# Routed expert slots: down products one slot later, up weights in halves, TensorE's order as called

## The chip, the cores and the metric

One core of a Trainium2 chip runs the whole program. The time is device microseconds of one execution. The engines are TensorE (PE: matrix products and transposes by a product with the identity), VectorE (DVE), ScalarE (ACT), GpSimd (POOL) and SyncE (SP), which here only sends transfers; ScalarE and GpSimd send some too. Each engine works through its own list of instructions in order, and waits there for what its next instruction needs.

## The reference, cut to what matters

A two-layer decoder on 4 x 512 tokens of width 512, each layer with gated cross attention and a gated feed-forward part. The part at stake is the first layer's feed-forward part, a mixture of experts: each token goes to its two best experts of 8, scaled by its score.

```python
scores = softmax(xf @ gate_w)                       # xf: 2048 x 512
_, sel = top_k(scores + expert_bias, 2)
order = argsort(sel.reshape(-1), stable=True)       # 4096 rows, by expert
token_idx = order // 2
routed_in = xf[token_idx] * top_scores_sorted[:, None]
h = silu(ragged_dot(routed_in, w1, counts)) * ragged_dot(routed_in, w3, counts)
routed_out = ragged_dot(h, w2, counts)              # w1, w3: 8 x 512 x 448, w2: 8 x 448 x 512
out = (silu(xf @ sw1) * (xf @ sw3)) @ sw2
out = out.at[token_idx].add(routed_out)
```

The second layer (a grouped attention with weights that were rounded to fp8, and a feed-forward part with weights of -1, 0 and 1) comes after it. Its weights are made ready while the slots run, and that is all of it that meets the change.

## The kernel before, in words

Tokens are scattered in DRAM to 39 slots of 128 rows, so that a slot's rows all belong to one expert (`owners` holds which). A loop runs over the slots; each slot `s` goes through four products on TensorE:

- `turn_in(s)` transposes the slot's rows: four 128x128 transposes into one PSUM tile of `ps_m` (2 buffers), copied to SBUF by `k.evac`. This helper gives its copies to VectorE (L120) and ScalarE (L122) in turn.
- `up(s)` multiplies them with the expert's two up matrices, tile `w13` (512 rows in four chunks of 128, times 2 x 448 columns, 1792 KB; two tiles, used by even and by odd slots): four chunks times two matrices, fp32, each as two passes. ScalarE takes the Silu of one result (L908), VectorE multiplies the other in (L909, the gate).
- `turn_hidden(s)` transposes the 448 hidden columns in four pieces of 112, with the same helper for the copy.
- `down(s)` multiplies with the expert's down matrix, tile `w2` (896 KB, two tiles). ScalarE scales the result into `m_y` (L927) and sends it to `slots_out` in DRAM (L928).

`load(s)` reads the slot's expert into a register of SP and sends for `w13`; `load_down(s)` sends for `w2`. Both are conditional from the third slot on: nothing is moved when slot `s - 2`, which used the same tile, had the same expert. So large transfers come only where an expert ends: with the loads of slots 0, 1, 16, 17, 18, 33 and 34. `load_rows(s)` sends for a slot's rows on ScalarE's queue, four slots ahead, into one of 7 buffers.

At the end of each round the loop calls steps of two lists of other work, which the second layer needs:

- `split`: steps that load a raw weight chunk (L1084, on SP), scale it (L1074), centre it (L1052 to L1054) on VectorE, round it on ScalarE (L1078), subtract on GpSimd (L1079), and store both halves by SP (L1080). One or two a slot.
- `ternary`: steps that load a 704 KB piece `t_raw` (L1807, on SP) and reduce it (L1814), two steps that make a scale from it with a small matmul (`t_pm`, L1824), and steps that turn a piece into codes (L1837 to L1839 on VectorE, a store by SP, L1840).

The order in which these calls become each engine's list is in most places that of a scheduler, which moves instructions where dependencies allow; in the attention stages a wrapper `Ordered` holds an engine's instructions in the order of the calls. In the slots of the kernel before, no such wrapper is used. There TensorE's list has early slots in the order hidden turn, row turn, up, down; late slots in the order up, hidden turn, row turn, down.

After the slots the program gathers each token's two rows from `slots_out`, adds them to `k.x`, and goes on to `context` (L989), the second layer's first products.

Of the kernel before, what the change touches and what calls it, by code (L numbers as in the profile page):

```python
# [22 lines left out]
P = 128  # L23
# [4 lines left out]
KC = D // P  # L28
# [5 lines left out]
E, HID, HC = 8, 448, 112  # L34
NHC = HID // HC
SLOTS = (2 * T + E * (P - 1)) // P
# [33 lines left out]
class Kernel:  # L70


    def __init__(self, ctx, tc, a, out):
        self.tc, self.nc, self.a, self.out = tc, tc.nc, a, out
        self.flip = 0
        nc = self.nc
        const = ctx.enter_context(tc.tile_pool(name="const", bufs=1))
        self.const = const
        self.small = ctx.enter_context(tc.tile_pool(name="small", bufs=4))

        self.x = const.tile([P, NT, D], F32, name="x_res")
        self.pcol = const.tile([P, NCOLS], F32, name="pcol_sb")
        self.rows = const.tile([P, NROWS], F32, name="rows_sb")
        nc.sync.dma_start(self.pcol, a["pcol"])
        nc.sync.dma_start(self.rows, a["rows"].partition_broadcast(P))

        self.ident = const.tile([P, P], F32, name="ident")
        make_identity(nc, self.ident)
        self.identb = const.tile([P, P], BF, name="identb")
        nc.vector.tensor_copy(self.identb, self.ident)  # L90
        self.ones = const.tile([P, P], F32, name="ones")
        nc.gpsimd.memset(self.ones, 1.0)
        self.neghalf = const.tile([P, 8], F32, name="neghalf")
        nc.gpsimd.memset(self.neghalf, -0.5)
        self.tg = const.tile([P, 4], F32, name="tg")
        nc.scalar.activation(self.tg, self.row("gates"), AF.Tanh)
# [534 lines left out]
        line.drain()  # L631


def moe(k, split, codes8, scratch, ffn):


# [9 lines left out]
    nc, tc, a = k.nc, k.tc, k.a  # L646
    with ExitStack() as ctx:
# [12 lines left out]
        w13 = [p1.tile([P, KC, 2, HID], F32, name=f"m_w13_{j}") for j in range(2)]  # L660
# [38 lines left out]
        for b in range(B):  # L699
            k.layernorm([(xn[b][:, t, :], k.x[:, b * TB + t, :]) for t in range(TB)])  # L700
            for c in range(KC):
                pt = ps_m.tile([P, S], F32, tag="ps_m")
# [44 lines left out]
        def by_token(name):  # L747
            return p1.tile([P, NT], F32, name=name)
# [34 lines left out]
        pt = ps_m.tile([P, 2, NT, E], F32, tag="ps_m", name="r_counts")  # L783
# [41 lines left out]
        for r, hot in enumerate(hots):  # L825
# [8 lines left out]
            s = by_token(f"r_s{r}")  # L834
# [22 lines left out]
        got = {}  # L857

        def load(s):


            e = got["e", s] = nc.values_load(
                owners[:, s : s + 1], engines=(mybir.EngineType.SP,), min_val=0, max_val=E - 1,
                skip_runtime_bounds_check_because="it is at most E - 1 by construction",
            )
            got["new", s] = None if s < 2 else e != got["e", s - 2]
            nc.sync.dma_start(w13[s % 2], a["w13"][e], cond=got["new", s])

        def load_rows(s):
            work = p6.tile([P, 4, D], F32, tag="m_big", name=f"m_work{s}")  # L870
            rows = nc.scalar.dma_start(work[:, 0, :], rows_in[ts(s, P), :])
            for scatter in scatters:
                tc.add_manual_dep(
                    rows.ins, scatter.name,
                    mybir.DependencyInfo(mybir.DependencyClass.Sync, mybir.DependencyReason.DATA),
                    reason="any of them may write a row of the slot",
                )

            tc.add_manual_dep(
                rows.ins, silus[B * NHC - NHC - 1].name,  # L880
                mybir.DependencyInfo(
                    mybir.DependencyClass.NoSync, mybir.DependencyReason.SCHED_ONLY
                ),
                reason="order of ScalarE's queue",
            )
            got["work", s] = work

        def load_down(s):
            nc.sync.dma_start(w2[s % 2], a["w2"][got["e", s]], cond=got["new", s])

        def turn_in(s):
            work = got["work", s]
            pt = ps_m.tile([P, KC, P], F32, tag="ps_m")
            for c in range(KC):
                nc.tensor.transpose(pt[:, c, :], work[:, 0, ts(c, P)], k.ident)
            k.evac(work[:, 1, :].rearrange("p (c t) -> p c t", c=KC), pt)

        def up(s):
            work, w = got["work", s], w13[s % 2]
            pu = ps_h.tile([P, HID], F32, tag="ps_h")  # L900
            pw = ps_h.tile([P, HID], F32, tag="ps_h")
            for c in range(KC):
                for half, pp in enumerate((pu, pw)):
                    nc.tensor.matmul(
                        pp, lhsT=work[:, 1, ts(c, P)], rhs=w[:, c, half, :],
                        start=(c == 0), stop=(c == KC - 1),
                    )
            nc.scalar.activation(work[:, 2, 0:HID], pu, AF.Silu)  # L908
            nc.vector.tensor_tensor(work[:, 2, 0:HID], work[:, 2, 0:HID], pw, ALU.mult)  # L909

        def turn_hidden(s):
            work = got["work", s]
            pt = ps_m.tile([P, NHC, P], F32, tag="ps_m")
            for m in range(NHC):
                nc.tensor.transpose(pt[:HC, m, :], work[:, 2, ts(m, HC)], k.ident)
            k.evac(work[:HC, 3, :].rearrange("p (c t) -> p c t", c=NHC), pt[:HC])

        def down(s):
            work, w = got.pop(("work", s)), w2[s % 2]
            po = ps_o.tile([P, D], F32, tag="ps_o")  # L920
            for m in range(NHC):
                nc.tensor.matmul(
                    po, lhsT=work[:HC, 3, ts(m, P)], rhs=w[:, m, :],
                    start=(m == 0), stop=(m == NHC - 1),
                )
            y = p4.tile([P, D], F32, tag="m_row", name=f"m_y{s}")
            nc.scalar.activation(y, po, AF.Copy, scale=k.tg[:, 2:3])  # L927
            nc.scalar.dma_start(rows_out[ts(s, P), :], y)  # L928
# [4 lines left out]
        for s in range(2):  # L933
            load(s)
            load_down(s)
        turn_in(0)
        up(0)
        turn_in(1)
        for s in range(SLOTS):
            if s + 1 < SLOTS:  # L940
                up(s + 1)
            turn_hidden(s)
            if s + 2 < SLOTS:
                load(s + 2)
                turn_in(s + 2)
            down(s)
            if s + 2 < SLOTS:
                load_down(s + 2)
            if s + 4 < SLOTS:
                load_rows(s + 4)  # L950
            for _ in range(-(-len(split) // (SLOTS - s))):
                split.pop(0)(ps)
            if ternary:
                ternary.pop(0)()


        kaff = p1.tile([P, 2], F32, name="kx_affine")
# [99 lines left out]
def split_weights(k):  # L1057
# [49 lines left out]
        steps += [partial(key_value, i, c) for c in range(KC)]  # L1107
        steps += [partial(project, i, src, h) for src in range(2) for h in range(HP)]
    return s, steps


class Ordered:


    def __init__(self, tc, engine):
        self.tc, self.engine = tc, engine

    def __getattr__(self, name):
        call = getattr(self.engine, name)
        return lambda *args, **kw: self.tc.keep_in_program_order(call(*args, **kw))  # L1120


class Beat:
# [16 lines left out]
    def load(self, tick, engine):  # L1140
        return self.loads.get((tick, engine), 0)
# [712 lines left out]
@with_exitstack  # L1854
def kernel(ctx: ExitStack, tc: tile.TileContext, a: dict, out: bass.AP):
    k = Kernel(ctx, tc, a, out)
    xattn_int8(k)
    scratch, split = split_weights(k)
    with tc.tile_pool(name="codes", bufs=1) as pool:
        codes8 = Codes(k, pool)  # L1860
        ffn = Ffn(k)
        first = moe(k, split, codes8, scratch, ffn)
        attend_and_feed(k, scratch, codes8, first, ffn)
# [85 lines left out]
```

## Time and profile before

| what | us |
|---|---|
| median of 3 runs | 3661.64 (3653.7 to 3664.58) |
| the profiled execution | 3658.38 |
| its span, first to last instruction | 3656.7 |
| mean granted TensorE clock | 0.965 |
| slot stage, first row turn to last down product (starts) | 868.6 to 1311.62 |

Times in the profile are from the start of the span. A line of the timeline gives the start, the duration, the engine, the line of the program, the operation, what it writes and reads, its shape and how many instructions of the kind follow one another; a bracket gives the idle time just before it and what ended it. A matmul's end is modelled, so of a row of matmuls the distance between starts is the better measure of their pace. "SPq" is SP's own queue, where a transfer's line gives the time at which it was sent, not how long it was under way. An fp32 product shows as two instructions.

### The profile page before, as it was taken

Reading aid. Unit: us, or ns where it says so; the run is one execution under the profiler, and the core shown is the slowest. Engines: PE = TensorE matmul, PEld = TensorE weight load, DVE = VectorE, ACT = ScalarE, POOL = GpSimd, SP = SyncE. Lnnn points to the kernel's source line nnn. Section 1 sums busy time; section 2 is a strip of 40 time slices with the busy share of each in tenths; the row PEclk is TensorE's granted clock in tenths of the full one; section 3 lists DMA queues with packets and bytes.
Section 4 is the critical chain, followed back from the end, with each engine's and each line's share of the span. In section 5 each row is a group of like instructions: output and inputs, shape, how many; then the busy total and the mean of one; then the engine's idle time right before and its main releaser. Section 6 shows DMA issues by size and latency. Waiting matters only on the chain.

```text
span 3656.7 us, 46871 instructions
## 1 busy us (share of the span) xinstructions
PE 3350.2 (92%) x15536; PEld 2193.1 (60%) x15552; DVE 2208.1 (60%) x4678; ACT 1507.4 (41%) x4198; POOL 1345.1 (37%) x1517
## 2 busy tenths in 40 slices
PE   6988987889999878889999999999999999999996
PEld 3544544434544433347777777776777777777774
DVE  6676676642143345635557767678766687666555
ACT  2544554111212211126555455554555554555542
POOL 1000000331001134524446654457545466544442
PEclk8999998989999989999999999999999999999998
DMA  5544442476265563343333242322332332332310
GB/s 179 153 113 113 121 110 60 173 242 215 104 208 174 203 225 115 134 140 100 103 104 104 81 141 90 121 96 94 117 124 90 116 104 98 113 110 95 105 50 14
DMA packets 223025, 452.85 MB, mean 124 GB/s; under 512 B 21440, under 2 KB 80320, under 8 KB 220224
## 3 DMA queue, kind: packets, MB, share of 16 engines
q1 hardware_dynamic: 206432, 412.62, 34.5%
q10 hardware_dynamic: 11232, 20.45, 1.7%
q0 software_dynamic: 5120, 16.78, 1.4%
q8 instruction: 125, 2.05, 0.2%
q14 instruction: 116, 0.95, 0.1%
HBM read 420.87 MB, written 116.98 MB: 147 GB/s over the span
## 4 chain that ended last, share of the span: by engine, by line
PE 47%; DVE 8%; POOL 2%; issue 2%; DMA 1%; ACT 1%; SPq 0%; DVEq 0%; POOLq 0%; ACTq 0%
PE ps_w L1120 10%; PE pss L1120 10%; PE ps_p L1120 9%; PE ps_o L1120 9%; PE ps_t L1120 7%; PE pk L989 2%; DVE y L1120 2%; DMA m_got<-slots_out,r_posi 1%; DVE nm L1120 1%; DVE g_hn L1120 1%; DVE t_work L1120 1%; DVE e L1120 1%; DVE g_pT L1120 1%; DVE t_sm L1120 0%; POOL g_rstd L1120 0%
## 5 line engine op out<-in xcount | busy, mean ns | idle before, releaser
L1120 PEld LDWEIGHTS ps_w<-g_pT,g_v 128*128 128x128 f32 x2048 | 388.1, 190 | 298.9 <-issue 222.2
L1120 PE MATMUL ps_w<-g_pT,g_v 128*128 128x256 f32 x2048 | 529.3, 381 | 23.3 <-DVE y L1120 12.5
L1120 ACT ACTIVATE g_p<-pss,nm 128x512 f32<-128x512 f32 x512 | 350.9, 685 | 479.0 <-DVE nm L1120 434.2
L1120 PE MATMUL pss<-g_kT,g_qT 128*128 128x512 f32 x1024 | 524.1, 594 | 0.9 <-ACT g_p L1120 0.9
L1120 POOL TENSOR_SCALAR g_p<-g_p,rs 128x512 f32<-128x512 f32 x512 | 368.6, 721 | 385.3 <-DVE rs L1120 366.1
L1120 DVE TENSOR_REDUCE nm<-pss 128x1 f32<-128x512 f32 x512 | 351.1, 686 | 105.7 <-PE pss L1120 104.5
L1120 PE MATMUL ps_t<-ident,g_p 128*128 128x128 f32 x2048 | 307.5, 273 | 0.0
L1120 PE MATMUL ps_o<-g_wp,g_cq 128*128 128x512 f32 x1024 | 286.4, 422 | 5.6 <-POOL g_cq L1120 3.0
L1079 POOL TENSOR_TENSOR hl<-raw,hl 128x512 fp32r<-128x512 f32 x80 | 102.0, 1282 | 512.0 <-ACT hl L1078 501.0
L1120 POOL TENSOR_TENSOR g_rstd<-ss,neghalf 128x4 f32<-128x4 f32 (+1 forms) x192 | 178.2, 928 | 303.8 <-ACT ss L1120 303.6
L1120 PE MATMUL ps_p<-g_wq,g_xq 128*128 128x512 f32 x1024 | 282.2, 417 | 6.5 <-DMA g_wq<-s_q 6.2
L1120 DVE COPY g_pT<-ps_t 128x512 f32<-128x512 f32 x246 | 168.4, 685 | 166.9 <-PE ps_t L1120 166.5
L1120 POOL TENSOR_TENSOR t<-y,c 128x512 f32<-128x512 bf16 x176 | 204.9, 1164 | 162.9 <-DVE c L1120 84.4
L1120 PEld LDWEIGHTS ps_t<-ident,g_p 128*128 128x128 f32 x2048 | 243.8, 141 | 26.0 <-POOL g_p L1120 0.9
L1120 ACT COPY g_pT<-ps_t 128x512 f32<-128x512 f32 x266 | 155.0, 583 | 231.6 <-PE ps_t L1120 231.2
L989 PE MATMUL pk<-m_wx,m_ctxT 128*128 128x512 f32 x512 | 239.7, 613 | 5.2 <-issue 5.2
L521 ACT ACTIVATE p<-pss,nm 128x512 f32<-128x512 f32 x256 | 175.4, 690 | 135.9 <-DVE nm L518 134.6
L1120 PEld LDWEIGHTS ps_o<-g_wp,g_cq 128*128 128x128 f32 x1024 | 195.8, 192 | 48.5 <-POOL g_cq L1120 3.5
L1120 PEld LDWEIGHTS ps_p<-g_wq,g_xq 128*128 128x128 f32 x1024 | 191.4, 190 | 50.0 <-issue 7.9
L518 DVE TENSOR_REDUCE nm<-pss 128x1 f32<-128x512 f32 x256 | 173.2, 688 | 71.0 <-PE pss L513 69.6
L1120 DVE RECIPROCAL rs<-g_sm 128x1 f32<-128x1 f32 x512 | 82.5, 161 | 205.2 <-ACT g_p L1120 203.2
L1120 ACT ACTIVATE junk<-ps_p 128x128 f32<-128x128 f32 x640 | 177.1, 277 | 67.3 <-PE ps_p L1120 53.1
(312 smaller groups left out, 6017.5 us busy)
## 6 DMA issues: line engine op xcount, KB each, us to landing
m_w<-in_w_dram SPq DMA_DIRECT2D x39, 1792.0 KB
g_wp<-s_proj SPq DMA_DIRECT2D x128, 512.0 KB
m_w<-in_w_dram SPq DMA_DIRECT2D x39, 896.0 KB
g_wq<-s_q SPq DMA_DIRECT2D x128, 256.0 KB
g_wq<-s_qx SPq DMA_DIRECT2D x128, 256.0 KB
st_k<-dhl_k SPq DMA_DIRECT2D x64, 256.0 KB
st_q<-dhl_q SPq DMA_DIRECT2D x64, 256.0 KB
s_proj<-hl SPq DMA_DIRECT2D x32, 512.0 KB
```

Source lines behind the costliest of these rows:

```text
L518: nc.vector.tensor_reduce(nm, pss, AX.X, ALU.max, negate=True)
L521: nc.scalar.activation(p, pss, AF.Exp, bias=nm, accum_out=sums[:, qt, n : n + 1])
L989: nc.tensor.matmul(pk, lhsT=ctxT[b][:, c, ts(t, P)], rhs=ws[i][:, c, :], start=(c == 0), stop=(c == KC - 1),)
L1079: nc.gpsimd.tensor_tensor(hl[:, 1, :], raw, hl[:, 0, :].bitcast(F32), ALU.subtract)
L1120: return lambda *args, **kw: self.tc.keep_in_program_order(call(*args, **kw))
```

## The change

It does three things in the slot loop.

1. TensorE's instructions in `turn_in`, `up`, `turn_hidden` and `down` go through `Ordered`, so that they stand in TensorE's list in the order of the calls. The class is moved up in the file, unchanged.
2. `down(s - 1)` is called in round `s`, behind `up(s + 1)` and ahead of `turn_hidden(s)`; the last one follows the loop. TensorE's list becomes: row turn 0, up 0, row turn 1, up 1, hidden turn 0, row turn 2; then in each round up(s + 1), down(s - 1), hidden turn(s), row turn(s + 2).
3. `w13` is sent for in two halves, chunks 0 and 1, then chunks 2 and 3, each under the same condition; and `load(s + 3)` comes right behind `up(s + 1)`, ahead of the down weights, where it was `load(s + 2)` behind `turn_hidden(s)`. Down weights follow `down(s - 1)`, which frees their tile.

```diff
         def load(s):
...
-            nc.sync.dma_start(w13[s % 2], a["w13"][e], cond=got["new", s])
+            for c in (0, KC // 2):
+                some = slice(c, c + KC // 2)
+                nc.sync.dma_start(w13[s % 2][:, some], a["w13"][e][:, some], cond=got["new", s])
...
+        PE = Ordered(tc, nc.tensor)
+
         def turn_in(s):
...
-                nc.tensor.transpose(pt[:, c, :], work[:, 0, ts(c, P)], k.ident)
+                PE.transpose(pt[:, c, :], work[:, 0, ts(c, P)], k.ident)
...
         def up(s):
...
-                    nc.tensor.matmul(
+                    PE.matmul(
...
         def turn_hidden(s):
...
-                nc.tensor.transpose(pt[:HC, m, :], work[:, 2, ts(m, HC)], k.ident)
+                PE.transpose(pt[:HC, m, :], work[:, 2, ts(m, HC)], k.ident)
...
         def down(s):
...
-                nc.tensor.matmul(
+                PE.matmul(
...
         turn_in(0)
         up(0)
+        load(2)
         turn_in(1)
         for s in range(SLOTS):
+
             if s + 1 < SLOTS:
                 up(s + 1)
+            if s + 3 < SLOTS:
+                load(s + 3)
+            if s:
+                down(s - 1)
+                if s + 1 < SLOTS:
+                    load_down(s + 1)
             turn_hidden(s)
             if s + 2 < SLOTS:
-                load(s + 2)
                 turn_in(s + 2)
-            down(s)
-            if s + 2 < SLOTS:
-                load_down(s + 2)
             if s + 4 < SLOTS:
                 load_rows(s + 4)
             for _ in range(-(-len(split) // (SLOTS - s))):
                 split.pop(0)(ps)
             if ternary:
                 ternary.pop(0)()
+        down(SLOTS - 1)
```

The wrapper:

```python
class Ordered:
    def __init__(self, tc, engine):
        self.tc, self.engine = tc, engine
    def __getattr__(self, name):
        call = getattr(self.engine, name)
        return lambda *args, **kw: self.tc.keep_in_program_order(call(*args, **kw))
```

More of the change, by code (lines that the diff above doesn't have):

```diff
@@ L631, in xattn_int8, with __init__, __getattr__ @@
         line.drain()
+class Ordered:
+    def __init__(self, tc, engine):
+        self.tc, self.engine = tc, engine
+    def __getattr__(self, name):
+        call = getattr(self.engine, name)
+        return lambda *args, **kw: self.tc.keep_in_program_order(call(*args, **kw))
 def moe(k, split, codes8, scratch, ffn):
@@ L1109, in split_weights @@
     return s, steps
[L1112 to L1120, printed above, removed]
 class Beat:
```

## The prediction

> **What bounds the kernel now.** First the busy table of the page, for the kernel as a whole:
>
> ```profile
> PE 3350.2 (92%) x15536; PEld 2193.1 (60%) x15552; DVE 2208.1 (60%) x4678; ACT 1507.4 (41%) x4198; POOL 1345.1 (37%) x1517
> ```
>
> TensorE is busy for 92% of the span, so only its work, its idle time and its clock count, and the change leaves its products as they are. What is left to win or lose lies in the stage of the routed slots: its first turn starts at 868.6 us, its last down product at 1311.6, so 443.0 us. The table of windows (PE, PEld, DVE, ACT and POOL busy, granted clock, DMA share, GB/s) shows three kinds of slot:
>
> ```profile
> 940.00:980.00 40.00, 39.28 (x123) 20.36 (x122) 7.43 (x13) 8.40 (x14) 2.53 (x2) 1.00 0.30 105
> 1180.00:1220.00 40.00, 35.91 (x110) 17.71 (x109) 7.62 (x14) 9.88 (x18) 7.58 (x6) 1.00 0.47 158
> 1220.00:1260.00 40.00, 31.06 (x80) 14.56 (x79) 14.15 (x23) 7.50 (x13) 7.60 (x6) 0.91 0.79 271
> ```
>
> Early slots have almost no idle TensorE (0.7 of 40 us); later ones lose 4.1 of 40; the stretch where new experts come loses 8.9, and clock too. The timeline of TensorE (start, duration, line, count, then in brackets the idle time before it and who ended that) says why. An early slot:
>
> ```profile
> 1004.42 0.60 PE L915 MATMUL pt<-ident,m_work 128*112 128x128 f32 x4
> 1004.86 0.60 PE L895 MATMUL pt<-ident,m_work 128*128 128x128 f32 x4
> 1005.29 0.92 PE L904 MATMUL pu<-m_w,m_work 128*128 128x448 f32 x2
> ...
> 1011.31 3.60 PE L922 MATMUL po<-m_w,m_work 112*128 112x512 f32 x8
> 1014.75 0.28 PE L1824 MATMUL t_pm<-tot,ones 128*128 128x1 f32 x2
> ```
>
> Nothing waits: the turns (L915 hidden, L895 rows) stand ahead of an up product (L904) that does not need them. A late slot, and the last one:
>
> ```profile
> 1279.57 0.92 PE L904 MATMUL pu<-m_w,m_work 128*128 128x448 f32 x2
> ...
> 1286.54 0.65 PE L915 MATMUL pt<-ident,m_work 128*112 128x128 f32 x4 [0.78 <-DVE m_work L909]
> 1287.02 0.60 PE L895 MATMUL pt<-ident,m_work 128*128 128x128 f32 x4
> 1287.86 3.70 PE L922 MATMUL po<-m_w,m_work 112*128 112x512 f32 x8 [0.24 <-ACT m_work L122]
> ...
> 1310.19 0.65 PE L915 MATMUL pt<-ident,m_work 128*112 128x128 f32 x4 [0.79 <-DVE m_work L909]
> 1311.62 0.70 PE L922 MATMUL po<-m_w,m_work 112*128 112x512 f32 x1 [0.78 <-DVE m_work L120]
> ```
>
> Here the hidden turn follows its own up product and waits for the gate (0.78), and the down product waits for the copy out of PSUM (0.24; 0.78 where nothing stands between). The next up starts at 1291.40: a pitch of 11.83 us. Last, the weights and the queues:
>
> ```profile
> 1236.28 1.02 PE L904 MATMUL pu<-m_w,m_work 128*128 128x448 f32 x2 [2.47 <-DMA m_w<-in_w_dram]
> ...
> 1252.77 1.86 PE L904 MATMUL pu<-m_w,m_work 128*128 128x448 f32 x2 [3.18 <-DMA m_w<-in_w_dram]
> ```
>
> ```profile
> 1053.30 0.46 SPq L1807 DMA_DIRECT2D t_raw<-in_w_gu_dram  x1
> 1063.48 0.95 DVE L1837 TENSOR_SCALAR t_raw<-t_raw,sc_w_gu 128x1408 f32<-128x1408 f32 x1 [8.06 <-DMA t_raw<-in_w_gu_dram]
> 1220.52 1.75 DVE L1054 TENSOR_TENSOR raw<-raw,m 128x512 f32<-128x512 f32 x1
> ```
>
> All waits for weights: 2.47 + 3.18, 1.48 for a down product at 1245.92 and 0.70 at 1047.6, in sum 7.8. After the last one the matmuls run at half clock (1.86 against 0.92); that up product takes 9.3 instead of 6.2, so 3.0 more. Deliveries cost 10.9 us of the stage.
>
> **The change part by part.** *Blocks.* From the early lines: an up product has a pitch of 6.02 (1005.29 to 1011.31), 6.12 where its first matmul had to wait; a down 3.44; hidden turn to row turn 0.44; row turn to up 0.43. A group of turns takes 0.60 by itself, and the copy behind it keeps a waiting product 0.78 by VectorE (1310.19 + 0.65 to 1311.62) or 0.68 by ScalarE (1298.36 + 0.65 to 1299.69).
>
> *TensorE's order as called, down one slot later.* The list becomes up(s+1), down(s-1), hidden turn(s), row turn(s+2), up(s+2). The gate of s and the hidden copy of s now lie behind a whole product: the 0.78 and 0.24 of late slots go. But each row turn is now followed at once by the up product that reads it, so its copy is exposed in every slot: L120, on VectorE in every slot by the alternation (hidden copies go to ScalarE). Pitch: 6.12 + 3.44 + 0.44 + 0.60 + 0.78 = 11.38. Before, it was 10.98 over the first 24 slots (down 0 at 883.26, down 24 at 1146.88) and 11.77 over the last 14 (164.7 / 14), all waits included. So 24 x 0.40 = 9.6 is lost and 14 x 0.39 = 5.5 won. Whole stage: head with three turns exposed to the third up product 16.8 (3 x (0.60 + 0.78) + 2 x 6.12 + 0.44); 36 x 11.38 = 409.7; tail up, down, hidden turn with ScalarE's 0.68, down, hidden turn with 0.78: 6.12 + 3.44 + 0.60 + 0.68 + 3.54 + 0.60 + 0.78 = 15.8. Sum 442.3 against 443.0: **-0.7**, with the waits for weights and the slow clock gone. An estimate: the halves bring the weights in time, since half a is sent some 3 us after an up product starts and needed two slots later (about 19 us), half b about 16; whole 1792 KB took 8.7 (1227.57 to 1236.28) and 11.0. If not, up to 6 of the 10.9 comes back.
>
> *Added instructions.* 39 more sends on SP, 0.33 to 0.36 where sent, 0.07 to 0.10 where skipped, with their register work: below 1 us of SP per slot of 11, and no engine waits for SP but through data: 0. Cover gone, each would delay a load by that much.
>
> *Wait added on VectorE's list.* The row copy stands behind what is queued between gate(s+1) and it. The copy can run about 10.5 after the slot's up product starts, the gate ends at about 6.9, so 3.6 us of other work is free. In about half of the slots nothing stands there. Eight coding instructions (L1837 to L1839, pitch 0.8 to 0.9) ahead of one copy: 0.4. Three code steps in slots 16 to 18 begin with a wait for `t_raw`, 704 KB, whose send stands on SP between or behind the weight halves of loads 16 to 18. In the trace such a piece landed 11.9 and 10.2 us after its send (1053.30 to 1063.48) beside weights, 4.6 and 5.3 alone. Landing in 5 costs 0, in 10 to 12 some 14 in sum; I take 6, as half of the weights now come in the other half of the slot. Other code slots: 0.3. Two split steps ahead of a late copy: a tie, 0.3.
>
> *Wait added on SP's list.* `w2` of slots 33 and 34 is now sent behind two stores of split halves, which wait for POOL: an estimate of 2.3 after the up product starts, needed at 6.1 by a down; it landed in 6.2 under load (1239.67 to 1245.92), 4.4 if it had the full rate of about 400 GB/s seen at 1028 to 1032. So 0.6 to 2.4 each; I take 1.3 for both, near the low end, since the up halves have by then mostly landed.
>
> *Two rules of the Trainium skill.* The row 1220.52 is 1.75 us long where the same instruction takes 0.68 elsewhere; POOL's subtract (1.27) runs beside it. "SBUF — State Buffer", section "Who interferes with whom", says that a VectorE instruction with two inputs in SBUF and a GpSimd one that reads SBUF exclude each other for a whole instruction. The copy L120, with PSUM as source, took 0.68 to 0.69 in all 39 slots, so it is not hit itself, but work ahead of it is. By the rule each split beside a subtract adds 1.07: three to six slots, 3 to 6 us. By the row's place (the long one comes after the copy in most slots) 0. I take 0 and keep 6 for the range. Second: "TensorE: Matmul & The Clock Gate", sections "What's actually happening" and "Part 4: PE-mode transpose", says that an idle window of about 3.4 us halves the clock and that turns do not count as busy. The new order has turns and a wait of 0.44 + 0.60 + 0.78 = 1.8 in a row per slot; the late slots before had 0.78 + turns 1.1 + 0.24 = 2.1 and a clock of 1.00 in 1180 to 1220. So by the trace 0; by the rule 0 too until the copy is late by over 1.6, and then some 3 to 6 for the slot. It speaks against this change wherever `t_raw` is late, and stands in the range.
>
> *Behind the stage.* The next stage has TensorE idle for 20 us before 1344, waiting on gathers that need the last slot's store; they follow the last down product 1:1. Later waits can move both ways as VectorE's list shifts; 0, with 5 each way.
>
> **Sum**: -0.7 + 0.4 + 6 + 0.3 + 0.3 + 1.3 = 7.6, two thirds of what could be told from no change. Against the profiled execution (span 3656.7, with 1.7 outside it 3658.4): 3666.0. The median of the runs shown is 3661.6, 3.3 above it; so **3669**.
>
> **The rivals.** *Slower: VectorE's head of line.* The row copies of slots 17 to 20 stand behind code steps that wait for `t_raw`. For: the bracket of 8.06 at 1063.48, and 391 to 400 GB/s in 1040 to 1060, so weights and pieces share a full pipe. Against: down weights now go after the piece, not before. Price: 14, and both down weights 5: -0.7 + 0.4 + 14 + 5 + 0.6 = 19.3, so 3681 against the median. It decides from the point where a piece lands later than 9.5 us after the slot's up product starts.
>
> *Faster.* Everything in time gives only -0.7; over 0.3% (11 us, about what a measurement of this kernel can tell from no change) is had only if the next stage gains too, for example if its norm work is drawn into the slots and the 20 us wait shrinks by half: -0.7 - 10 = 3651. For: that wait is real. Against: it follows the last store, which the change does not advance.
>
> *It does not do what it says.* SP's stores hold the halves as they held the whole, so weights are late again: 7.6 + 6 = 13.6, 3675.
>
> **How the numbers follow.** Forecast case (within about 6 of 3669) 0.45; head of line 0.27; not doing what it says 0.13; faster 0.15, of which a part stays within 0.3%. Bounds: 3661.6 - 11 to 3661.6 + 11 is 3651 to 3673; part of the forecast case and half of the third lie above. So faster 0.13, same 0.47, slower 0.40. The range takes in the head of line with the shared-port price (19 + 6) and, below, the faster case: 3651 to 3687.
>
> **What the profile after would show.** Right: in every slot 0.78 of idle before the first L904 matmul (its line moved), by VectorE's row copy; no gate waits before hidden turns; no wait on weights in 1220 to 1260, clock 1.00; pitch 11.4 early and late; first turn to last down 448 to 450. Head of line: 3 to 5 us before the up products of slots 17 to 19, half clock behind them, VectorE waiting on `t_raw`. Wrong: waits of the up products for weights, an early pitch still at 11.0, or a change behind 1345 larger than 5.

## The result: 0.2% slower, and the profile after

| | before | after |
|---|---|---|
| median of 15 runs, us | 3661.0 | 3668.2 |
| ratio, 95% interval | | 1.0021 (1.0011 to 1.0030) |
| span of the profiled execution, us | 3656.7 | 3669.4; 3668.7 in a second profile |
| slot stage: first row turn to last down product (starts), us | 443.0 | 459.5; 452.3 |
| from the last down product to the last product of `context` (starts), us | 300.5 | 301.6; 300.7 |
| from that product to the last group of matmuls (starts), us | 2036.5 | 2034.6; 2034.6 |

The single executions of the changed kernel lie between 3655 and 3678 us, those of the kernel before between 3653 and 3665. The loss is in the slot stage. The first profile started the slots 3.0 us earlier than before, the second 4.5 later; the change doesn't touch the work that stands there, and why their start moves stays open. Of the changed kernel, TensorE's instructions in the slots all stand at L642, the wrapper's line, so they are told apart by tiles: `pt` turns, `pu` and `pw` up, `po` down.

The busy table of its page, and the windows of the slots, in the same columns as before:

```profile
PE 3346.9 (91%) x15536; PEld 2192.5 (60%) x15552; DVE 2197.9 (60%) x4678; ACT 1503.5 (41%) x4198; POOL 1342.7 (37%) x1517
```

```profile
940.00:980.00 40.00, 37.65 (x112) 19.09 (x112) 9.68 (x19) 8.13 (x14) 5.03 (x4) 1.00 0.37 125
1180.00:1220.00 40.00, 36.87 (x116) 19.21 (x115) 4.78 (x8) 9.56 (x17) 7.51 (x6) 1.00 0.46 162
1220.00:1260.00 40.00, 37.65 (x114) 19.04 (x113) 15.18 (x29) 8.02 (x15) 5.03 (x4) 1.00 0.70 237
1262.00:1300.00 38.00, 28.21 (x70) 13.35 (x69) 9.07 (x22) 5.98 (x11) 6.62 (x6) 0.87 0.59 187
```

The work is the same (3350.2 to 3346.9 us busy), so it is idle time that grew. Early slots lost busy time (39.28 to 37.65 of 40), late ones won a little (35.91 to 36.87), the stretch from 1220 is whole again with its clock (31.06 to 37.65). But the lost time came back behind it: 1262 to 1300 has 9.8 us idle and a clock of 0.87. The timeline of TensorE shows the new wait, an early slot first, then slot 18:

```profile
1002.33 3.60 PE L642 MATMUL po<-m_w,m_work 112*128 112x512 f32 x8
1005.77 1.04 PE L642 MATMUL pt<-ident,m_work 128*112 128x128 f32 x8
1007.59 1.02 PE L642 MATMUL pu<-m_w,m_work 128*128 128x448 f32 x2 [0.78 <-DVE m_work L120]
...
1062.71 1.04 PE L642 MATMUL pt<-ident,m_work 128*112 128x128 f32 x8
1066.35 1.33 PE L642 MATMUL pu<-m_w,m_work 128*128 128x448 f32 x2 [2.59 <-DVE m_work L120]
1067.47 1.70 PE L642 MATMUL pw<-m_w,m_work 128*128 128x448 f32 x2
```

Hidden turn and row turn are one group of 8, and the up product behind them waits for the row copy: 0.78, in all but a few slots. The pitch (from the start of one up product to the start of the next) is 11.37 to 11.38 in 29 of the 38 steps. In slot 18 the copy is late. VectorE's timeline says why, and SyncE's when the piece was sent:

```profile
1055.26 0.42 SPq L1816 DMA_DIRECT2D t_raw<-in_w_gu_dram  x1
...
1062.88 0.95 DVE L1846 TENSOR_SCALAR t_raw<-t_raw,sc_w_gu 128x1408 f32<-128x1408 f32 x1 [2.71 <-DMA t_raw<-in_w_gu_dram]
1063.87 0.90 DVE L1847 TENSOR_SCALAR t_raw<-t_raw 128x1408 f32<-128x1408 f32 x1
1064.80 0.89 DVE L1848 TENSOR_SCALAR t_raw<-t_raw 128x1408 fp8e4<-128x1408 f32 x1
1065.61 0.68 DVE L120 COPY m_work<-pt 128x512 f32<-128x512 f32 x1
```

The copy could have run at about 1063.7, when the turns were done, and stood behind three instructions of a code step that had waited for its piece. This is the head of line of the prediction, in one slot instead of three. And the down products of slots 33 and 34, with SyncE's sends (L902 is the down weights, L1100 the stores of split halves) and the down product of slot 31 ahead of them:

```profile
1244.79 3.60 PE L642 MATMUL po<-m_w,m_work 112*128 112x512 f32 x8
1252.14 0.09 SPq L902 DMA_DIRECT2D m_w<-in_w_dram  x1
...
1262.37 1.56 SPq L1100 DMA_DIRECT2D s_qx<-hl  x2
1264.34 0.36 SPq L902 DMA_DIRECT2D m_w<-in_w_dram  x1
...
1271.33 5.37 PE L642 MATMUL po<-m_w,m_work 112*128 112x512 f32 x8 [3.48 <-DMA m_w<-in_w_dram]
...
1289.38 6.77 PE L642 MATMUL po<-m_w,m_work 112*128 112x512 f32 x8 [4.74 <-DMA m_w<-in_w_dram]
```

The tile of slot 33's down weights came free at about 1248.4, when the down product of slot 31 ended. They were sent 16 us later, at 1264.3: SyncE's list had fallen behind by more than a slot (the send at 1252.14 is slot 32's, skipped, for a tile that was free at 1237.0), and between 1250 and 1264 it still had to wait for POOL before the two stores of 512 KB at 1262.37. For slot 34 the gap is 21.5 us. Slot 33's weights then took 7.0 us to land. 5.37 and 6.77 instead of 3.6 for the products themselves: half clock behind the wait.

### The profile page after: what moved, and what is told of

Same layout as the page of the kernel before. It is cut to its first block, busy times and chain, and to the rows that moved or that the text cites. A ratio compares the mean times of both kernels' runs of the same rounds, so it can differ in the third digit from the quotient of the medians.

```text
span 3669.4 us, 47131 instructions
## 1 busy us (share of the span) xinstructions
PE 3346.9 (91%) x15536; PEld 2192.5 (60%) x15552; DVE 2197.9 (60%) x4678; ACT 1503.5 (41%) x4198; POOL 1342.7 (37%) x1517
## 4 chain that ended last, share of the span: by engine, by line
PE 69%; DVE 14%; DMA 6%; issue 4%; POOL 3%; ACT 3%; SPq 0%; POOLq 0%; DVEq 0%; ACTq 0%
PE ps_w L642 10%; PE pss L642 10%; PE ps_p L642 9%; PE ps_o L642 9%; PE ps_t L642 7%; PE pu L642 3%; PE po L642 3%; PE pw L642 3%; PE pk L1009 3%; PE po L543 3%; PE pt L535 2%; DVE y L642 2%; PE pss L513 2%; PE pk L478 2%; DMA m_got<-slots_out,r_posi 2%
## 5 line engine op out<-in xcount | busy, mean ns | idle before, releaser
L642 PEld LDWEIGHTS ps_w<-g_pT,g_v 128*128 128x128 f32 x2048 | 388.2, 190 | 298.4 <-issue 221.9
L642 PE MATMUL ps_w<-g_pT,g_v 128*128 128x256 f32 x2048 | 529.5, 381 | 22.8 <-DVE y L642 12.3
L642 ACT ACTIVATE g_p<-pss,nm 128x512 f32<-128x512 f32 x512 | 350.6, 685 | 478.2 <-DVE nm L642 437.7
L642 PE MATMUL pss<-g_kT,g_qT 128*128 128x512 f32 x1024 | 524.1, 594 | 0.9 <-ACT g_p L642 0.9
L642 POOL TENSOR_SCALAR g_p<-g_p,rs 128x512 f32<-128x512 f32 x512 | 366.7, 717 | 386.7 <-DVE rs L642 361.5
L642 DVE TENSOR_REDUCE nm<-pss 128x1 f32<-128x512 f32 x512 | 350.5, 685 | 106.1 <-PE pss L642 104.8
L642 PE MATMUL ps_t<-ident,g_p 128*128 128x128 f32 x2048 | 307.5, 273 | 0.0
L642 PE MATMUL ps_o<-g_wp,g_cq 128*128 128x512 f32 x1024 | 286.3, 422 | 5.6 <-POOL g_cq L642 3.0
L642 POOL TENSOR_TENSOR g_rstd<-ss,neghalf 128x4 f32<-128x4 f32 (+1 forms) x192 | 178.0, 927 | 302.9 <-ACT ss L642 302.9
L642 PE MATMUL ps_p<-g_wq,g_xq 128*128 128x512 f32 x1024 | 281.6, 416 | 6.6 <-DMA g_wq<-s_q 6.2
L642 DVE COPY g_pT<-ps_t 128x512 f32<-128x512 f32 x246 | 168.3, 684 | 167.6 <-PE ps_t L642 167.3
L642 POOL TENSOR_TENSOR t<-y,c 128x512 f32<-128x512 bf16 x176 | 204.5, 1162 | 162.8 <-DVE c L642 83.6
L642 PEld LDWEIGHTS ps_t<-ident,g_p 128*128 128x128 f32 x2048 | 243.8, 141 | 26.2 <-POOL g_p L642 1.1
L642 ACT COPY g_pT<-ps_t 128x512 f32<-128x512 f32 x266 | 154.8, 582 | 232.1 <-PE ps_t L642 231.7
L642 PEld LDWEIGHTS ps_o<-g_wp,g_cq 128*128 128x128 f32 x1024 | 195.8, 191 | 48.5 <-POOL g_cq L642 3.5
L642 PEld LDWEIGHTS ps_p<-g_wq,g_xq 128*128 128x128 f32 x1024 | 191.1, 190 | 50.1 <-issue 8.0
L642 DVE RECIPROCAL rs<-g_sm 128x1 f32<-128x1 f32 x512 | 82.3, 161 | 204.9 <-ACT g_p L642 203.0
L642 ACT ACTIVATE junk<-ps_p 128x128 f32<-128x128 f32 x640 | 176.7, 276 | 66.2 <-PE ps_p L642 52.0
```

## The experiments

All times are medians against the kernel before on the same chip (3659.2 to 3659.8 in each group).

**Row turn ahead of the down product.** From the changed kernel:

```diff
+            if s + 2 < SLOTS:
+                turn_in(s + 2)
             if s:
                 down(s - 1)
                 if s + 1 < SLOTS:
                     load_down(s + 1)
             turn_hidden(s)
-            if s + 2 < SLOTS:
-                turn_in(s + 2)
```

> The changed kernel with one thing moved: the row turn of slot s+2 is called right behind the up product of s+1, ahead of the down product of s-1, so that its copy lies beside down product and hidden turn. My theory (the new wait of 0.78 plus 0.26 by the copy is the price of the order): the wait goes in all slots, pitch 6.02 + 3.44 + 0.44 + 0.44 = 10.3 to 10.4 instead of 11.38, so 36 x 1.0 = 36 off the stage; some 10 of it may be lost again in waits for weights, which have less time: 3635 to 3648. Rival (VectorE's other work and the weights set the pace, and the copy's wait only stands in for them): other waits grow by as much, 3660 to 3668.

3638.4, ratio 0.9946 (0.9929 to 0.9964); stage 424.3. TensorE's timeline of a slot of it, to its next up product (a small matmul of a scale step, 0.15 us of pace, stands ahead of that one):

```profile
1010.37 0.60 PE L642 MATMUL pt<-ident,m_work 128*128 128x128 f32 x4
1010.81 3.60 PE L642 MATMUL po<-m_w,m_work 112*128 112x512 f32 x8
1014.25 0.60 PE L642 MATMUL pt<-ident,m_work 128*112 128x128 f32 x4
1014.68 0.28 PE L1833 MATMUL t_pm<-tot,ones 128*128 128x1 f32 x2
1014.83 1.00 PE L642 MATMUL pu<-m_w,m_work 128*128 128x448 f32 x2
```

No bracket: the copy runs beside the down product. The pitch is 10.32 to 10.33 where nothing is late, the sum of the blocks without a wait (6.02 + 3.44 + 0.44 + 0.43), and the waits for weights grew only to 13.5 (8.4 at down, 5.1 at up products; 8.2 and 0 in the changed kernel). So the exposed row copy is the price of the change's order: 36 slots at 1.05, 38 us; the stage is 35.2 and 28.0 shorter than in the two profiles of the changed kernel. This move changed VectorE's list too, and code steps no longer delay an up product; but the 10.33 of the quiet slots comes out of the order alone.

**TensorE's order as called, nothing else.** The kernel before with its four functions through the wrapper:

```diff
+        PE = Ordered(tc, nc.tensor)
...
-                nc.tensor.transpose(pt[:, c, :], work[:, 0, ts(c, P)], k.ident)
+                PE.transpose(pt[:, c, :], work[:, 0, ts(c, P)], k.ident)
```

> The kernel before with TensorE's order held as called and nothing else: up of s+1, hidden turn of s, row turn of s+2, down of s. Then the gate lies behind a whole up product and the row copy behind a down product; only ScalarE's hidden copy stands exposed, for 0.24 behind the row turn. My theory: pitch 6.02 + 1.27 + 3.54 = 10.8 in all slots against 10.98 and 11.77, weights late as before: 38 x 10.8 = 411 against 428 - 11, so -6, 3655 (range 3648 to 3660). Rival (the planner's order is as good): within 3 us of the kernel before.

3646.0, ratio 0.9957 (0.9943 to 0.9971). Pitch 10.82 to 10.83 and stage 435.6, 7.4 less than before, as worked out (-6). The total fell by 14, more than expected; the rest is behind the slots, 292.1 us against 300.5; the first context was sent at 1304.1 instead of 1314.1, and what hangs on that comes below. Holding an order is not what cost time; this order leaves 0.24 exposed, the change's order 0.78 and the turn before it.

**The load part alone.** The kernel before with `w13` in halves, and:

```diff
+        load(2)
         turn_in(1)
...
                 up(s + 1)
+            if s + 3 < SLOTS:
+                load(s + 3)
             turn_hidden(s)
             if s + 2 < SLOTS:
-                load(s + 2)
                 turn_in(s + 2)
```

> The kernel before with the load part of the change alone: up weights in halves, sent for right behind the next slot's up call, two slots ahead; TensorE's order free, down in its old round. The planner then lays TensorE's list as up, hidden turn, row turn, down in 32 of the slots, not in the last 14 only. My theory (a slot's cost is set by which copy or gate stands exposed between two products, and weights are a separate term): the waits of up products for weights (5.7 us in the last slots, 0.7 in the early ones) go, but the gate's 0.78 and the copy's 0.24 come into some 18 more slots, so +18 x 0.8 = +14, less 10.9: 3658 to 3668. Rival (weights are what matters): about -10, 3651.

3648.7, ratio 0.9958 (0.9943 to 0.9973), stage 431.1: my theory missed and the rival was right in size. I had misread the planner's list: where I saw up, hidden turn, row turn, down of one slot, the up product is that of the next slot. Its pitch is 10.83 in most slots, as with the order held, with gate waits in 6 slots only (13 before). So this run isn't the load part alone: moving a load made the planner lay TensorE's list anew. What it does show is that waits of up products for weights nearly go (0.7 us against 6.4), while two down products wait 5.4.

**The load part left out.** The changed kernel with `w13` whole, and:

```diff
-        load(2)
...
-            if s + 3 < SLOTS:
-                load(s + 3)
...
             if s + 2 < SLOTS:
+                load(s + 2)
                 turn_in(s + 2)
```

> The changed kernel without its load part: TensorE's order as called and down one slot later, but up weights whole and sent for in their old place behind the hidden turn. My theory: pitch 11.38 as in the changed kernel, the two waits of down products for weights (8.2 us and the slow clock behind them) get smaller and waits of up products for whole weights come back, 2 to 4 us each in slots 33 and 34: within 6 us of the changed kernel, 3662 to 3674. Rival (the halves cause the whole loss): back at or below the kernel before, 3661 or less.

3797.7, ratio 1.0373 (1.0360 to 1.0387): neither. With that load later, the planner drew the split steps into the early slots (on VectorE's list nearly all stand in slots 4 to 13). Two lines of TensorE in that stretch:

```profile
958.40 1.86 PE L642 MATMUL pu<-m_w,m_work 128*128 128x448 f32 x2 [14.29 <-DVE m_work L120]
980.13 1.86 PE L642 MATMUL pu<-m_w,m_work 128*128 128x448 f32 x2 [9.65 <-DVE m_work L120]
```

Row copies behind split steps that wait for raw chunks, sent by a SyncE that itself waits: 79.2 us of waits for the copy and 68.7 for up weights (15.5 of it in slots where no weights are moved; this comes with the two combinations), stage 602.6. As a separation of the parts the run is void; as a measure of how far the head of line can go it is the largest number here.

**Up weights whole, in the early place.** From the changed kernel:

```diff
-            for c in (0, KC // 2):
-                some = slice(c, c + KC // 2)
-                nc.sync.dma_start(w13[s % 2][:, some], a["w13"][e][:, some], cond=got["new", s])
+            nc.sync.dma_start(w13[s % 2], a["w13"][e], cond=got["new", s])
```

> The changed kernel with up weights sent whole again, but in the new, early place. My theory: halves do nothing by themselves, since half a was sent some 20 us ahead of its use and whole weights took 8.7 to 11: no wait of an up product for weights, time within 5 us of the changed kernel (3663 to 3673), unless the planner moves the split steps. Rival (halves are what brings weights in time): waits of 2 to 3 us at up products of slots 16 to 18, 33 and 34, 3673 to 3680.

3683.5, ratio 1.0063 (1.0049 to 1.0076), above the ranges of both. One up product waits for weights (2.7 us; none in the changed kernel), row copies wait 33.5 instead of 30.2, since split and code steps again stand elsewhere on VectorE's list, and the stage behind takes 305.5 instead of 301.6. Its profile is 12.5 us longer than the first one of the changed kernel: 3.5 ahead of the slots, 3.5 in them, 3.9 behind them to the last product of `context`, 1.5 after that. Only the one wait of 2.7 can be put down to the whole weights; the rest came with the other places of the steps, so what halves are worth by themselves stays open.

**Down weights ahead of the stores.** Stores of split halves are kept back until the next down weights are sent:

```diff
-        nc.sync.dma_start(to, hl.bitcast(F32))
+        held.append(lambda: nc.sync.dma_start(to, hl.bitcast(F32)))
...
-                    load_down(s + 1)
+                    sent = load_down(s + 1)
+                    while split_weights.held:
+                        tc.add_manual_dep(
+                            split_weights.held.pop(0)().ins, sent.ins.name,
```

> The changed kernel with one order on SyncE turned round: the stores of the split halves go behind the next down weights, not ahead of them. In the changed kernel's trace the down weights of slots 33 and 34 were sent 2.8 us after the up product's start, behind two stores of 512 KB, and landed 7.0 and 8.1 later; the two down products waited 8.2 us and ran slow behind it (13 in all). My theory: sent right when the down product before frees the tile, ahead of those stores, they land in 4.4 to 6: waits of 0 to 1, so 11 to 13 off the stage, 3654 to 3659; what may be lost is in the split steps, whose stores and raw loads come later. Rival (the pipe is full whatever the order): waits stay within 3 us of 8.2, time within 4 us of the changed kernel.

3680.1, ratio 1.0053 (1.0039 to 1.0067). The waits went and the time did not fall: no down product waits for weights any more (8.2 to 0). Slot 33's weights were sent 4.8 us ahead of the up product before their use instead of 2.8 behind its start, though still 11 after their tile came free. So their place on SyncE's list was the cause, as far as this run can show it: its slots are longer too, which gives SyncE time. In the next run, with slots of 11.48, the sends go out at once and no product waits for weights. But the planner now laid split steps with code steps in slots 23 to 29, and row copies wait 48.2 us instead of 30.2. (The slots began at 834.2 instead of 865.6 and took 492.0; what left the stage ahead of them stays open.)

**Row copies on ScalarE, hidden copies on VectorE.** From the changed kernel:

```diff
+        k.flip ^= 1
         turn_in(0)
```

> The changed kernel with the two kinds of copies exchanged: row copies on ScalarE, hidden copies on VectorE. My theory: the exposed copy is now ScalarE's, 0.68 instead of 0.78, so pitch 11.28 (-4 in all), and it no longer stands behind code steps that wait for t_raw, so slot 18 loses its 3.5: about -7, 3659 to 3664. Rival (the wait is TensorE's own turn-to-product time, not the copy): pitch stays 11.38, time as the changed kernel.

3642.4, ratio 0.9952 (0.9938 to 0.9965). The pitch went up by 0.1 instead of down: ScalarE has its own list, here with the scaling of the down product and its send ahead of the copy. The copy's bracket names the turns, but those were done at 1013.7 (1012.68 and 1.04 on TensorE); the send was over at 1013.95.

```profile
1012.88 0.69 ACT L942 ACTIVATE m_y<-po,tg 128x512 f32<-128x512 f32 x1 [1.51 <-PE po L642]
...
1013.59 0.36 ACTq L943 DMA_DIRECT2D slots_out<-m_y  x1
1013.99 0.59 ACT L122 COPY m_work<-pt 128x512 f32<-128x512 f32 x1 [0.43 <-PE pt L642]
```

The stalls by code steps went, and no weights are waited for (those of slots 33 and 34 were sent 0.03 and 0.75 us after their tiles came free): stage 452.5. Most of the gain is behind the slots: 281.2 us against 301.6, which neither the theory nor the rival had.

**What the stage behind waits for.** In the changed kernel its first product waits for the transposed context, which SyncE sends last:

```profile
1333.48 1.55 SPq L1100 DMA_DIRECT2D s_proj<-hl  x2
...
1337.61 0.83 SPq L1051 DMA_DIRECT2D m_ctxT<-in_ctxT_dram  x1
...
1345.75 9.33 PE L1009 MATMUL pk<-m_wx,m_ctxT 128*128 128x512 f32 x16 [16.98 <-DMA m_ctxT<-in_ctxT_dram]
```

The last split steps stand ahead of it, and their stores wait for POOL. With row copies on ScalarE the first context was sent at 1302.7, some 15 us ahead of the last down product. To test this, split steps were called over the first 31 slots:

```diff
-            for _ in range(-(-len(split) // (SLOTS - s))):
+            for _ in range(-(-len(split) // max(1, SLOTS - 8 - s))):
```

> The changed kernel with the split steps called over the first 31 slots instead of all 39, so that their stores and raw loads are through before slots 33 and 34 and before the stage behind. My theory (down weights are late only because two stores of 512 KB go ahead of them; the stage behind takes 300 us from the last down product to its last product where split stores stand ahead of the context loads on SyncE, 281 where they don't): the 13 us at slots 33 and 34 go, and up to 20 in the stage behind; row copies behind split and code steps in slots 25 to 30 may give back up to 15: 3635 to 3652. Rival (the stage behind follows the last store, whatever SyncE does): only the 13, 3655.

3668.2, ratio 1.0027 (1.0014 to 1.0040), the time of the changed kernel. Both gains are there: 280.7 us behind the slots (-21), down weights in time. Both are eaten in slots 25 to 30, where split and code steps now stand ahead of the row copy: 44.6 us of waits for it. TensorE, and VectorE ahead of that wait:

```profile
1165.63 0.95 DVE L1846 TENSOR_SCALAR t_raw<-t_raw,sc_w_dn 128x1408 f32<-128x1408 f32 x1
1166.61 1.84 DVE L1847 TENSOR_SCALAR t_raw<-t_raw 128x1408 f32<-128x1408 f32 x1
1168.48 1.83 DVE L1848 TENSOR_SCALAR t_raw<-t_raw 128x1408 fp8e4<-128x1408 f32 x1
1170.24 0.68 DVE L120 COPY m_work<-pt 128x512 f32<-128x512 f32 x1
...
1170.97 1.86 PE L642 MATMUL pu<-m_w,m_work 128*128 128x448 f32 x2 [7.01 <-DVE m_work L120]
```

**The same in the kernel before.**

> The kernel before with nothing changed but that the split steps are called over the first 31 slots. My theory: the late slots lose their stores, so of the 10.9 us of late weights some 7 go, the stage behind gains up to 20, TensorE's free order may move either way by 5: 3632 to 3650. Rival (the gain needs the new order): within 5 us of the kernel before.

3663.5, ratio 1.0008 (1.0000 to 1.0016): the rival's time, not by its reason. 284.0 behind the slots (-16.5), stage 462.1 (+19), of it gate waits of 28.5 us against 10.2. With the run above it shows that in both orders 16 to 21 of the 300 us go when the split steps end earlier. That this works through SyncE's list is seen in the changed kernel, which waits for the context. The kernel before had its first context product at 1320.53 and then waited 14.76 for VectorE's norm of it, behind the adds of gathered rows; there the path is not shown.

**Two combinations.** Row turn first, with down weights ahead of stores:

> Row turn ahead of the down product (which gave 3638), and down weights ahead of the stores on SyncE. My theory: pitch 10.33 as there, and of its 13.5 us of waits for weights (8.4 at down, 5.1 at up products) and the slow clock behind them most of the 8.4 goes: 3623 to 3632, the fastest of all. Rival (what is won in the slots is lost in the stage behind, where gathers and context weights are late): within 4 us of 3638.

3660.5, ratio 1.0002 (0.9992 to 1.0011). Not as thought: up products wait 36.6 us for weights in 12 places, down products 7.6 (8.4 with the row turn alone). More than half of these waits are for weights that are not moved at all. Slots 24 to 27 have the expert of the slots before them, so their sends are skipped, but a product still waits until SyncE has come to the skipped send:

```profile
1101.00 0.34 SPq L1863 DMA_DIRECT2D ffn_codes<-t_raw  x1
...
1106.67 0.60 SPq L880 DMA_DIRECT2D m_w<-in_w_dram  x2
1106.87 1.83 PE L642 MATMUL pu<-m_w,m_work 128*128 128x448 f32 x2 [6.26 <-DMA m_w<-in_w_dram]
```

The tile was free at 1086.0. SyncE stood ahead of a store of codes, which waits for VectorE, until 1101.0, and had stores and loads of the split steps next. Such waits make 17.5 of the 36.6 us and 7.2 of the 7.6.

Row turn first, row copies on ScalarE, split steps early:

> The changed kernel with three things: row turn ahead of the down product, row copies on ScalarE and hidden copies on VectorE, split steps over the first 31 slots. My theory: no copy is exposed (pitch 10.33), no row copy stands behind VectorE's steps, down weights of slots 33 and 34 come in time, the stage behind starts with its loads sent: stage 412 to 420 and 281 behind, 3612 to 3622. Rival (weights and split steps collide earlier instead): waits for weights of 10 or more in other slots, 3630 to 3640.

3638.5, ratio 0.9954 (0.9933 to 0.9975), inside the rival's range. 276.0 behind the slots, pitch 10.33 in quiet slots, but weights (18.4 us, 14.5 of it for skipped sends) and copies (6.7) wait in slots 19 to 34, stage 440.9. It is no better than the row turn alone. With 3638 us the two are the best versions found, 0.5% ahead of the kernel before and 0.8% ahead of the changed one (3638.4 against 3668.2).

**The changed kernel once more.**

> The changed kernel once more, unchanged, for a second profile: how far its terms repeat. The pitch of 11.38 and the sum of the row copies' waits (30.2) should repeat within 0.5; the waits of down products in slots 33 and 34 (8.2) and of the first product of the stage behind (17.0), which hang on transfers, may differ by some us each.

One execution, 3670.5. Row copies wait 30.2 us again, and the first product behind the slots 16.7 for the context. The down weights' waits are 6.4 instead of 8.2, and the wait in slot 18 is 2.03 instead of 2.59, without half clock.

## Why the prediction was right

The time was forecast as 3669 and is 3668.2. The step that carries the argument, the exposed row copy in every slot, is shown by the pitch and by the run that moves the row turn; no hidden turn waits for a gate, and 1220 to 1260 has no wait for weights and a clock of 1.00, as it said. That the time fits to 1 us is in part luck. The stage was forecast at 448 to 450 us and measured at 459.5 and 452.3; the two profiled executions are 12.7 and 12.0 longer than the one before, not 7.6, while the medians are 7.2 apart. Two terms of the stage were off, one too large and one too small, and the work after `context` is 1.9 shorter.

- *Pitch*: worked out as 11.38, measured 11.37 to 11.38. The head took 16.9 (16.8 forecast). The quiet stage, -0.7, stands: in the first profile 443.0 - 0.7 + 13.6 (down weights: pitches of 11.52, 16.79 and 19.45 less 11.38 each) + 3.5 (slot 18: 13.19 and 13.07) = 459.4, and 459.5 was measured; in the second 443.0 - 0.7 + 8.6 + 1.3 = 452.2, and 452.3 was measured.
- *Halves in time*: no up product waits for weights; the 7.8 us of waits and the slow clock at the old places went.
- *Code steps behind `t_raw`*: 6 taken, 3.5 and 1.3 measured. The two pieces that VectorE waited for in slots 17 and 18 landed in 5.9 and 7.6 us, between the 5 and the 10 to 12 that I had weighed, and only slot 18 was hit.
- *Down weights behind stores*: this term was mis-sized. 1.3 taken, up to 4.8 allowed, 13.6 and 8.6 measured. The late send was right (2.8 us after the up product's start; 2.3 was worked out). Landing was taken as 4.4 to 6.2; it took 7.0 and 8.1, with two stores of 512 KB sent just ahead, two raw chunks just behind, and the transfer engines busy for 0.94 and 0.85 of these stretches. (How the 4.4 was reached is not clear: 896 KB at 400 GB/s are 2.3.) And half clock behind each wait was left out, which makes about 5 of the 13.6; in the second profile one of the two waits had it, for 1.8.
- *Behind the stage*: 0 taken; +1.1 and +0.2 measured. But the sameness is chance. Before, TensorE had products early and then waited 14.8 for VectorE's `m_hn`, which stood behind gathers; after, it waits 17.0 for the context. The prediction named the gathers alone and said that they follow the last down product; the runs with split steps early show 16 to 21 us there that do not.
- *Clock rule*: "late by over 1.6" as the point from which half clock sets in fits slot 18 in both profiles: 2.59 in all (1.81 late) had it, 2.03 (1.25 late) had not. It does not hold elsewhere: with down weights ahead of the stores, a copy late by 1.28 had it and one late by 2.41 had not (lines in the last section). Whether turns count as busy time is not shown.
- *Added instructions*: 0 taken, as no engine waits for SP but through data; no up product waits for weights in the changed kernel, so 0 stands here. The reason is too narrow: products wait for skipped sends too, as the combinations show.
- *Shared port*: 0 taken; no wait in the changed kernel is traced to it. It costs where steps are dense, as the 1.84 us lines above show.
- *Rival, head of line*: it happened in one slot, at 3.5 and 1.3 of the 14 us that it was priced at, and far beyond its price with other placements of the split steps. The full pipe that spoke for it (391 to 400 GB/s in 1040 to 1060) had a gap: 296 from 1048 to 1052.

## What to carry to other kernels

A turn, its copy and the product that reads it must not be neighbours: put a product between them, and count for each order which copy stands exposed, since that term repeats in every slot (1.05 us in 36 slots here) while late weights cost a few slots. What stands on a queue ahead of a rare large transfer (a store that waits for another engine) is part of that transfer's price, with its bytes and with the slow clock behind the wait; and a transfer that a condition skips still has its place on the queue, and its reader waits until the queue gets there. Where a planner lays the lists, moving one send can move everything: read each engine's list of a variant before believing that it tests one thing.

## What the runs showed of the hardware

- VectorE's code operations took 0.89 us alone and 1.84 beside POOL's subtracts, and two subtracts then took 3.89 instead of 2.5 (in the run with split steps early, beside the VectorE lines shown there):

```profile
1165.68 3.89 POOL L1099 TENSOR_TENSOR hl<-raw,hl 128x512 fp32r<-128x512 f32 x2 [9.96 <-ACT hl L1098]
```

Both become longer, and it is not bound to instructions with two inputs, as the prediction had it: these have one tensor as input. The times fit two engines that take turns, a whole instruction at a time: from 1165.63 to 1170.31 there is room for 0.95 + 0.89 + 0.89 of VectorE and two subtracts of 0.98 each (an estimate from these lines, not tested).
- The length of a wait alone does not tell whether the clock drops. With down weights ahead of the stores, an up product after a wait of 2.06 us started at half clock (1.86 for two instructions), one after a wait of 3.19 at full, and stayed there; both stood behind a group of eight turns:

```profile
1125.43 1.86 PE L642 MATMUL pu<-m_w,m_work 128*128 128x448 f32 x2 [2.06 <-DVE m_work L120]
...
1171.64 1.02 PE L642 MATMUL pu<-m_w,m_work 128*128 128x448 f32 x2 [3.19 <-DVE m_work L120]
```

Over the slots of all 14 kept traces, each of the 34 waits of 3.39 us or more ahead of an up or down product was followed by half clock, at a price of 1.6 to 3.2 us; of the 29 waits between 2.0 and 3.37, 13 were.
